# The last attention of an eight-stage block: both batch elements' head quartets in one branch, and the second element's projections, values and routing spread over it

## The chip, the cores and the metric

The kernel runs on one core of one Trainium2 chip. A core has five engines, each with an instruction stream of its own: TensorE (PE; its weight loads are shown as PEld), VectorE (DVE), ScalarE (ACT), GpSimd (POOL) and SyncE (SP), which here only issues DMAs. The metric is the device time of one execution in microseconds (us); lower is better. The time before is the median of three runs.

## The reference, cut to what matters

x has two elements of 512 tokens by 512 channels (float32). Eight stages follow one another, each as x = x + stage(layernorm(x)). Only the last two are touched: a causal attention of 32 heads of 16 channels with rotary positions, and a feed-forward stage in which a router picks two of eight low-rank experts for each token (this stage is also run ahead of the attention, with the same weights).

```python
def _L1_attn_b_ref(hidden_states, qkv_w, qkv_b, out_w, out_b):
    qkv = hidden_states @ qkv_w + qkv_b
    q, k, v = jnp.split(qkv, 3, axis=-1)          # 32 heads of 16
    q = _rope(q, cos, sin)
    k = _rope(k, cos, sin)
    scores = jnp.einsum('bqhd,bkhd->bhqk', q, k) * scale
    scores = scores + (1.0 - causal) * MASK_VAL   # -66504
    probs = jax.nn.softmax(scores, axis=-1)
    ctx = jnp.einsum('bhqk,bkhd->bqhd', probs, v).reshape(b, s, e)
    return ctx @ out_w + out_b

def _L1_ffn_ref(x, W_base, b_base, W_router, A, B):
    logits = x_flat @ W_router.T
    probs = jax.nn.softmax(logits, axis=-1)
    topk_probs, topk_idx = jax.lax.top_k(probs, 2)
    topk_probs = topk_probs / jnp.sum(topk_probs, axis=-1, keepdims=True)
    combine = jnp.einsum('nk,nke->ne', topk_probs, onehot)
    hw = jnp.einsum('nd,erd->ner', x_flat, A) * combine[:, :, None]
    return x_flat @ W_base.T + b_base + jnp.einsum('ner,eor->no', hw, B) * 2
```

## The kernel before, in words

Tokens lie in tiles of 128 (four to an element, t = 0..3 for element 0 and 4..7 for element 1), x stays in SBUF, and `xT[b]` holds the layernormed element b transposed, channels in partitions. A line number is that of the kernel before.

**Projections** (`prepare`, L1770). For element b, `rotated` (L1747) makes q and then k in four tiles of 128 channels (eight heads) by 512 tokens: a chain of four products on TensorE (L176), on ACT the bias (L1755), on DVE a shuffle of the halves of each head (L1757) and the product with the sine table into `t2` (L1758), on POOL the product with the cosine table (L1759) and the sum (L1760). `t2` is a tile of the pool's tag "qm". Then DMAs (L1764) store the tile's heads into `rooms.q` and `rooms.kk`, where a *quartet* u (four heads) has a plane of its own, each head in the first 16 of 32 partitions. A spare partition of every head carries the row maximum into the second score product. `values(b)` (L1781) makes v token tile by token tile; DVE adds the bias (L1785). Between q and k of element 0 come the layernorms of element 1's tiles; between q and k of element 1 comes `experts.begin()` (L1611): for the four tiles of element 0, whose attention is then complete, a layernorm, the added bias, and `front` (L1544), the router: one chain, and some fifteen small DVE instructions that end with the weighted rows `hw` (L1568).

**Quartets** (`core`, L1792). Each of the eight quartets of an element takes 16 scores (S; `score` L1813: TensorE, four widths of 128 to 512 keys; DVE adds the mask and reduces the row maximum, L1823), a transposition of these maxima (M; `maxima` L1837, and their sum with q on DVE, L1839), 16 transposed scores (T; `transposed` L1849, exponential on ACT L1859, the diagonal cut on POOL L1863), the product with v (`values` L1874, copied by ACT L1882), and a division (L1888 to L1892). After the eight quartets the context is transposed (L1906) and copied (L1910, DVE and ACT in turn) and multiplied by the output weights; `add_to_x` (L237) adds the result to x on DVE.

**What sets the order.** TensorE's order within `core` is written out by hand (`run_ordered`, L361): eight scores ahead, then for each quartet the string below, in which `|` is the division of the quartet before; scores run ahead of the quartet whose transposed scores are due, so 24 scores stand before the first T (the *fill*), and the last quartets of an element have no scores left to issue. The other engines' order, and that outside `core`, is set by a planner from the program's order and its costs. Scores, products and transpositions take the eight PSUM banks in turn (`turn`, BANKS).

```python
order = "STTSTSSTSTTSTSTSTTTTS|TTSTMTSSSSSS"
...
for b in range(B):
    prepare(b)
    with tc.If(exact != 0) as branch:
        core(b, True)
    with branch.Else():
        core(b, False)
```

`exact` tells at run time whether the masked scores can be left out; if not, the Else branch works on all of them. There is one such branch per element. After the second, `Experts.end` (L1618) runs `back` (L1577) for each tile of element 0, layernorms and routers of element 1, their `back`, and the stores of the result. `HeadRooms` (L1690) owns the planes of q, k and v, and fills their spare parts on POOL during the experts' first run.

Of the kernel before, what the change touches and what calls it, by code (L numbers as in the profile page):

```python
# [39 lines left out]
P = 128  # L40
NT = S // P
# [5 lines left out]
class Block:  # L47


    def __init__(self, ctx, tc, x, out):  # L50
# [10 lines left out]
        self.held = None  # L61
# [66 lines left out]
    def proj(self):  # L128
        return self.bank("pj", 2)

    def tr(self):
        return self.bank("tp", 2)

    def sc(self):
        return self.bank("sc", 3)

    def av(self):
        return self.bank("av", 1)
# [14 lines left out]
    def hold(self):  # L153


        self.holding = ExitStack()
# [6 lines left out]
    def release(self, ctx):  # L163
        self.holding.close()
        self.held = None
        self.psum = ctx.enter_context(
            self.tc.tile_pool(name="psum", bufs=2, space=bass.MemoryType.PSUM)
        )
# [1519 lines left out]
class HeadRooms:  # L1688
# [5 lines left out]
    def __init__(self, k, a, pool):  # L1694
# [9 lines left out]
        self.nm = [one([P, NT, P], f"nm{i}") for i in range(2)]  # L1704

    def fill(self, i):
        pool = self.k.nc.gpsimd
        pool.memset(self.q[:, i], 0.0)
# [6 lines left out]
def attn_mha(k, a, exact, rooms, experts):  # L1715
# [9 lines left out]
    with ExitStack() as ctx:  # L1725
# [8 lines left out]
        bv = k.load_row(a["h_bv"], D, "h_bv", pool=lp)  # L1734
# [3 lines left out]
        v_of = lambda kc, head: v[:, (kc * H + head) * 17 : (kc * H + head) * 17 + 32]  # L1738
# [7 lines left out]

        def rotated(b, w, bias, out, queues):  # L1747
# [3 lines left out]
            for tt in range(T):  # L1751
                ps = k.proj()
                last = k.chain(ps, [(w[:, c, bass.ts(tt, P)], k.xT[b][:, c]) for c in range(KC)])
                y = full[:, tt]
                nc.scalar.activation(y, ps, AF.Identity, bias=bias[:, tt : tt + 1], scale=1.0)  # L1755
                t2 = lp.tile([P, S], F32, tag="qm", name="t2")
                nc.vector.stream_shuffle(t2, y, swap)  # L1757
                nc.vector.tensor_tensor(t2, t2, tables["sin"], ALU.mult)  # L1758
                nc.gpsimd.tensor_tensor(y, y, tables["cos"], ALU.mult)  # L1759
                nc.gpsimd.tensor_tensor(y, y, t2, ALU.add)  # L1760
# [20 lines left out]
        def values(b):  # L1781
            for t in range(NT):
                ps = k.sc()
                k.chain(ps, [(k.xT[b][:, c, bass.ts(t, P)], wv[:, c]) for c in range(KC)])
                nc.vector.tensor_tensor(  # L1785
                    v[:, t * H * 17 : (t + 1) * H * 17].rearrange("p (h d) -> p h d", d=17)[:, :, 0:16],
                    ps.rearrange("p (h d) -> p h d", d=16),
                    bv.rearrange("p (h d) -> p h d", d=16),
                    ALU.add,
                )  # L1790

        def core(b, causal):  # L1792
# [3 lines left out]
            if not causal:  # L1796


                wide = S + (NT - 1) * P
                add = lp.tile([P, wide], F32, tag="add", name="add", bufs=1)  # L1800
                addT = lp.tile([P, wide], F32, tag="addT", name="addT", bufs=1)
                for m, sign in ((add, 1), (addT, -1)):
                    nc.gpsimd.memset(m, 0.0)
                    nc.gpsimd.affine_select(
                        out=m, in_=m, compare_op=ALU.is_ge, fill=masked,
                        base=sign * (S - P), pattern=[[-sign, wide]],
                        channel_multiplier=sign,
                    )

            def score(u, qt, g):  # L1810
                kv = (qt + 1) * P if causal else S
                ps = k.turn()
                nc.tensor.matmul(  # L1813
                    ps[:, :kv],
                    q[rows[g], u, bass.ts(qt, P)],
                    kk[rows[g], u, :kv],
                    start=True,
                    stop=True,
                )
                at = 32 * g + spare  # L1820
                lo = S - (qt + 1) * P
                mask = k.mask if causal else add
                nc.vector.tensor_tensor_reduce(  # L1823
                    out=ps[:, :kv],
                    in0=ps[:, :kv],
                    in1=mask[:, lo : lo + kv],
                    op0=ALU.add,
# [88 lines left out]
        for b in range(B):  # L1916
            prepare(b)
            with tc.If(exact != 0) as branch:
                core(b, True)
# [190 lines left out]
```

## Time and profile before

| | us |
|---|---|
| median of three runs | 2051.23 (2049.56 to 2051.96) |
| the profiled execution | 2050.64 |
| its span in the profile | 2048.9 |
| mean granted TensorE clock in it | 0.987 |
| first score of element 0 / of element 1, start | 1729.9 / 1898.2 |
| values of the eight quartets, element 0, first start and last end | 1749.1 / 1819.45 |
| the same, element 1 | 1916.4 / 1986.97 |
| output products of element 1, end | 2003.0 |

How the profile is read: times count from the start of the span. PE, DVE, ACT and POOL are the engines; a name with q (SPq) is an engine's DMA and control queue, PEld the weight loads of TensorE. L176 is a line of the kernel. An instruction's line shows its start, its duration, the operation, "out<-in" by the program's names with partitions x elements, how many, and in brackets the idle time of its engine before it and who ended that. A windows line shows a stretch, its length, then each engine's busy time and instructions, the granted TensorE clock (1.00 is full), the DMAs' share and GB/s.

### The profile page before, as it was taken

Reading aid. Unit: us, or ns where it says so; the run is one execution under the profiler, and the core shown is the slowest. Engines: PE = TensorE matmul, PEld = TensorE weight load, DVE = VectorE, ACT = ScalarE, POOL = GpSimd, SP = SyncE. Lnnn points to the kernel's source line nnn. Section 1 sums busy time; section 2 is a strip of 40 time slices with the busy share of each in tenths; the row PEclk is TensorE's granted clock in tenths of the full one; section 3 lists DMA queues with packets and bytes.
Section 4 is the critical chain, followed back from the end, with each engine's and each line's share of the span. In section 5 each row is a group of like instructions: output and inputs, shape, how many; then the busy total and the mean of one; then the engine's idle time right before and its main releaser. Section 6 shows DMA issues by size and latency. Waiting matters only on the chain. (4 is left out here: it accounts for less than half of the span.)

```text
span 2048.9 us, 39076 instructions
## 1 busy us (share of the span) xinstructions
PE 1974.3 (96%) x15064; PEld 1107.5 (54%) x15064; DVE 1333.1 (65%) x3510; ACT 759.0 (37%) x2094; POOL 1003.5 (49%) x1288
## 2 busy tenths in 40 slices
PE   9899989999999999999999999999999989997999
PEld 5333346666666666666665545454544544654654
DVE  8779657656665566566664586666666675845854
ACT  3776622222232223222222264454445211641451
POOL 4411046675645567666653266646555544225121
PEclk9999999999999999999999999999999999999999
DMA  3010222122221222222221321020101003002001
GB/s 136 11 42 1 73 74 85 56 78 90 95 74 51 80 76 82 77 92 79 73 86 40 115 66 47 2 76 2 62 12 43 6 6 47 2 2 36 7 2 42
DMA packets 69784, 108.85 MB, mean 53 GB/s; under 512 B 13522, under 2 KB 50386, under 8 KB 62548
## 3 DMA queue, kind: packets, MB, share of 16 engines
q1 hardware_dynamic: 68660, 103.10, 16.1%
q8 instruction: 122, 2.00, 0.4%
q10 hardware_dynamic: 640, 1.05, 0.3%
q0 software_dynamic: 288, 2.10, 0.3%
q14 instruction: 74, 0.61, 0.1%
HBM read 80.00 MB, written 4.19 MB: 41 GB/s over the span
## 5 line engine op out<-in xcount | busy, mean ns | idle before, releaser
L282 ACT ACTIVATE room<-room,nmax 128x128 f32<-128x128 f32 (+3 forms) x384 | 212.1, 554 | 481.7 <-DVE nmax L272 480.7
L261 PE MATMUL held<-kT,q 128*32 128x64 f32 (+15 forms) x4096 | 264.7, 397 | 15.2 <-DVE invs L290 12.4
L293 POOL TENSOR_SCALAR room<-room,invs 128x128 f32<-128x128 f32 (+3 forms) x384 | 198.3, 536 | 153.3 <-DVE invs L290 153.3
L176 PE MATMUL held<-w,ctxT 128*128 128x512 f32 x512 | 228.8, 595 | 0.1
L272 DVE CUSTOM_DVE_ANT_0 room<-held,mask 128x128 f32<-128x128 f32 (+3 forms) x384 | 176.0, 487 | 65.6 <-PE held L261 62.0
L261 PEld LDWEIGHTS held<-kT,q 128*32 128x32 f32 x4096 | 142.5, 110 | 106.5 <-issue 28.8
L333 PE MATMUL held<-turned,vals 32*128 32x384 f32 (+7 forms) x2784 | 192.8, 421 | 2.1 <-DMA vals<-v 2.1
L570 DVE TENSOR_REDUCE nm<-held 128x1 f32<-128x512 f32 x256 | 161.7, 683 | 32.2 <-PE held L600 26.6
L333 PEld LDWEIGHTS held<-turned,vals 32*128 32x128 f32 (+1 forms) x2784 | 153.2, 169 | 39.9 <-issue 18.9
L176 PEld LDWEIGHTS held<-w,ctxT 128*128 128x128 f32 x512 | 94.7, 190 | 115.8 <-issue 108.4
L237 DVE TENSOR_TENSOR x<-held,x 128x512 f32<-128x512 f32 x120 | 81.5, 684 | 114.9 <-PE held L176 95.0
L306 DVE STREAM_TRANSPOSE turned<-room 128x1152 f32<-128x1152 f32 x80 | 109.2, 1366 | 43.5 <-POOL room L293 40.0
L1067 POOL TENSOR_TENSOR q<-q,cosq 128x512 f32<-128x512 f32 x60 | 89.4, 1491 | 59.7 <-DVE t L1064 59.7
L176 PE MATMUL held<-fold,ctxT 128*128 128x512 f32 x256 | 117.8, 604 | 0.5 <-ACT ctxT L347 0.5
L229 POOL TENSOR_TENSOR rstd<-ve,mhalf 128x1 f32<-128x1 f32 x64 | 36.8, 579 | 160.6 <-DVE ve L227 160.6
L282 ACT ACTIVATE probs<-probs,nmax 128x128 f32<-128x128 f32 (+3 forms) x128 | 71.1, 556 | 67.3 <-DVE nmax L272 66.1
L1023 PE MATMUL held<-room,w 128*128 128x256 f32 x384 | 95.1, 384 | 0.0
L293 POOL TENSOR_SCALAR probs<-probs,invs 128x128 f32<-128x128 f32 (+3 forms) x128 | 66.0, 535 | 58.9 <-DVE invs L290 56.9
L176 PE MATMUL sc<-w,room 128*128 128x512 f32 x208 | 92.7, 592 | 0.0
L1068 POOL TENSOR_TENSOR q<-q,t 128x512 f32<-128x512 f32 x64 | 88.0, 1374 | 6.5 <-DVE q L1067 2.5
L305 DVE STREAM_TRANSPOSE turned<-room 128x128 f32<-128x128 f32 x80 | 24.3, 304 | 101.3 <-POOL room L293 101.1
L1023 PEld LDWEIGHTS held<-room,w 128*128 128x128 f32 x384 | 71.4, 190 | 32.3 <-issue 21.6
(333 smaller groups left out, 4425.0 us busy)
## 6 DMA issues: line engine op xcount, KB each, us to landing
w<-in_b_wq SPq DMA_DIRECT2D x16, 1024.0 KB, 4.8
w<-in_b_wo SPq DMA_DIRECT2D x16, 1024.0 KB, 5.0
vals<-v SPq DMA_DIRECT2D x256, 64.0 KB, 2.0
w<-in_m_wo SPq DMA_DIRECT2D x8, 1024.0 KB, 4.8
w<-in_b_wk SPq DMA_DIRECT2D x16, 256.0 KB, 2.6
w<-in_b_wupv SPq DMA_DIRECT2D x16, 256.0 KB, 2.6
w<-in_m_wqn SPq DMA_DIRECT2D x8, 384.0 KB, 3.0
x<-in_x SPq DMA_DIRECT2D x8, 256.0 KB, 4.1
```

The source lines that it names most:

```text
L176: last = self.nc.tensor.matmul(out, lhsT, rhs, start=(i == 0), stop=(i == len(pairs) - 1))
L237: self.latest = self.nc.vector.tensor_tensor(self.x[t], ps, self.x[t], ALU.add).ins
L261: nc.tensor.matmul(ps[32 * i : 32 * i + 32, a - lo : b - lo], q[:, at : at + 32], keys[:, a:b], start=True, stop=True,)
L272: nc.vector.tensor_tensor_reduce(out=row, in0=ps[:, :kv], in1=self.mask_back[:, :kv] if qt % 2 else self.mask[:, S - kv :], op0=ALU.add, o ...
L282: nc.scalar.activation(row, row, AF.Exp, bias=nmax, scale=-1.0, accum_out=total[:, qt : qt + 1])
L293: self.nc.gpsimd.tensor_scalar(row, row, inv[:, qt : qt + 1], 1.0, ALU.mult, ALU.mult)
L306: self.nc.vector.transpose(out[:, :last], probs[:, :last])
L333: self.nc.tensor.matmul(out[:, :, :n], values(i, j), rhs, start=(j == blocks[0]), stop=(j == stop[i]),)
L570: k.latest = nc.vector.tensor_reduce(nm[u % 2][:, qt, at : at + 1], ps, AX.X, ALU.max, negate=True).ins
L1023: nc.tensor.matmul(out, lhsT[:, c], rhs[:, c], start=c == 0, stop=c == 1)
L1067: mul.tensor_tensor(q, q, tables["cosq"], ALU.mult)
L1068: nc.gpsimd.tensor_tensor(q, q, t2, ALU.add)
```

## The change

In the causal branch both elements' quartets run as one list of sixteen, n = 0..15, in one branch, which also holds `Experts.end`; the second `If` and all that stood between the two is gone from between them. The Else branch holds both elements one after the other, as before.

- `k.hold()` after `prepare(0)`: from there all eight banks are one held tile, and `proj`, `tr` and `sc` take the next bank in turn. `t2` takes the two buffers of the layernorm's "xn" instead of those of "qm".
- `HeadRooms` has four more planes (`more`), for q and k of the second element's first two quartets; the others reuse planes whose quartet of element 0 is done (`place`). POOL fills them in the experts' first run, with two memsets and two copies.
- The fill: two scores, then a projection tile of element 1, four times (q and k for heads 0 to 15), sixteen stores to `more` after the first two, ten scores, the maxima, six scores. The other sixteen stores of these tiles are issued after quartet 1.
- After quartet 7, `between`: the four remaining projection tiles with three scores after each and 32 stores, maxima of quartet 9, POOL's memsets of the places of element 1's v (in the space of wq and wk), the division, the first v tile, three scores, the context's transposition of element 0, its four output products with two scores after each, then three v tiles, the four layernorms and three of the four routers. The fourth router comes after quartet 8.
- The rotated tiles of element 1 lie in `xT[0]`, and so does the turned context of element 0: the four copies of the context follow the stores of the four tiles of `between`.
- Quartets 0 to 7 carry 16 scores each, and the maxima one quartet ahead; quartets 8 to 15 carry what is left, with the maxima two ahead.

The diff, cut to its core:

```diff
     def proj(self):
-        return self.bank("pj", 2)
+        return self.bank("pj", 2) if self.held is None else self.turn()
...
+        self.more = one([P, 4, S], "more")
...
+        def turn_pairs(y, ps, bias):
+            nc.scalar.activation(y, ps, AF.Identity, bias=bias, scale=1.0)
+            t2 = k.work.tile([P, S], F32, tag="xn", name="t2")
+            nc.vector.stream_shuffle(t2, y, swap)
+            nc.vector.tensor_tensor(t2, t2, tables["sin"], ALU.mult)
+            nc.gpsimd.tensor_tensor(y, y, tables["cos"], ALU.mult)
+            nc.gpsimd.tensor_tensor(y, y, t2, ALU.add)
...
+            flat = lambda w: w.rearrange("p c d -> p (c d)")
+            late, last = flat(wq)[:, : 3 * H * 17 + 32], flat(wk)[:, : H * 17 + 32]
+            ctxT = k.xT[0], wv
+            place = lambda b, u: u if b == 0 else u - 2 if u > 1 else 8 + u
+            q_of = lambda n: q[:, n] if n < 8 else rooms.more[:, n - 8]
+            k_of = lambda n: kk[:, n] if n < 8 else rooms.more[:, n - 6]
...
+            ys = [k.xT[0][:, i] for i in range(4)]
+            stored = {}
+
+            def rotated_tile(kind, tt):
+                w, bias = (wq, bq) if kind == "q" else (wk, bk)
+                ps = k.turn()
+                k.chain(ps, [(w[:, c, bass.ts(tt, P)], k.xT[1][:, c]) for c in range(KC)])
+                y = ys[(2 * tt + (kind == "k")) % 4]
+                turn_pairs(y, ps, bias[:, tt : tt + 1])
+                stored[kind, tt] = y
+
+            def store(tt):
+                for kind, of in (("q", q_of), ("k", k_of)):
+                    y = stored.pop((kind, tt))
+                    for n in range(8):
+                        at = 32 * (n % 4)
+                        nc.sync.dma_start(
+                            out=held(1, 2 * tt + n // 4, of)[at : at + 16],
+                            in_=y[16 * n : 16 * n + 16],
+                        )
...
+            def between():
...
+                for tt in (2, 3):
+                    for kind in "qk":
+                        rotated_tile(kind, tt)
+                        next_scores(3)
+                    store(tt)
+                maxima(9)
+                nc.gpsimd.memset(late, 1.0)
+                nc.gpsimd.memset(last, 1.0)
+                divided(7)
+                value_tile(0)
+                next_scores(3)
+                for c in range(T):
+                    turn_context(ctxts[0], ctxT[0], c)
+                for t in range(NT):
+                    output(0, t)
+                    next_scores(2)
+                experts.added = experts.bias()
+                for t in range(NT):
+                    if t:
+                        value_tile(t)
+                        next_scores(1)
+                    k.layernorm(t, bias=experts.added)
+                    if t:
+                        experts.front(t - 1)
+
+            ORDER = "STTSTSSTSTTSTSTSTTTTS|TTSTMTSSSSSS", "STTSTSSTSTTSTSTSTTTTS|TTSTTMSSSSSS"
             with tc.manual_schedule(engines={mybir.EngineType.PE}):
...
+                for tt in range(2):
+                    for kind in "qk":
+                        next_scores(2)
+                        rotated_tile(kind, tt)
+                    if tt == 0:
+                        store(0)
+                next_scores(10)
+                maxima(0)
+                next_scores(6)
+                for n in range(16):
...
+                    values_of(n)
+                    if n == 1:
+                        store(1)
+                    if n == 7:
+                        between()
+                    if n == 8:
+                        experts.front(NT - 1)
+                divided(15)
...
+            experts.end()
+
+        prepare(0)
+        k.hold()
+        with tc.If(exact != 0) as branch:
+            causal()
+        with branch.Else():
+            core(0)
+            prepare(1)
+            core(1)
+            experts.end()
```

## The prediction

> **What bounds the kernel now.** I read the page's busy shares first: TensorE is busy 96% of the span, so only two things can shorten it, less work on TensorE (the change removes none) or less of the 4% in which it stands.
>
> ```profile
> PE 1974.3 (96%) x15064; PEld 1107.5 (54%) x15064; DVE 1333.1 (65%) x3510; ACT 759.0 (37%) x2094; POOL 1003.5 (49%) x1288
> ```
>
> Then the windows view, cut at the stages of the last attention. Columns: stretch, length, busy time and instructions of each engine, granted TensorE clock, DMA share, GB/s.
>
> ```profile
> 1686.90:1729.90 43.00, 42.92 (x111) 19.32 (x111) 16.61 (x33) 7.52 (x12) 28.77 (x20) 1.00 0.36 55
> 1729.90:1740.10 10.20, 7.68 (x54) 5.51 (x56) 9.76 (x43) 0.00 (x0) 0.00 (x0) 0.81 0.02 4
> 1740.10:1821.40 81.30, 80.92 (x795) 49.71 (x791) 60.45 (x240) 49.76 (x137) 20.40 (x32) 0.98 0.01 2
> ...
> 1835.50:1849.30 13.80, 13.80 (x34) 6.07 (x33) 8.62 (x21) 2.06 (x3) 7.81 (x8) 1.00 0.01 2
> 1849.30:1868.90 19.60, 8.15 (x50) 7.17 (x48) 17.11 (x67) 3.69 (x9) 11.13 (x9) 0.83 0.37 52
> 1868.90:1884.30 15.40, 15.40 (x32) 6.69 (x33) 5.45 (x16) 2.06 (x3) 7.65 (x5) 0.89 0.03 3
> 1884.30:1898.20 13.90, 13.90 (x37) 5.91 (x35) 3.51 (x6) 0.69 (x1) 4.54 (x4) 1.00 0.51 77
> 1898.20:1908.60 10.40, 8.00 (x60) 6.00 (x62) 10.31 (x47) 0.00 (x0) 0.00 (x0) 0.92 0.00 0
> ```
>
> They are: projections of element 0; its fill (24 scores before the first transposed score); its eight quartets; then, for element 1, q projection, layernorms with routers, k projection, v, fill. Both fills run at DVE's pace (9.76 of 10.20), and in the routers' stretch TensorE stands 19.60 - 8.15 = 11.45 us while DVE works 17.11. The waits view says the same of the routers:
>
> ```profile
> PE pj L176 <- DVE cand L1537: 10.2, 2, 7.7
> ```
>
> What can be won is thus 11.45 (routers) + 2.4 (second fill) + 15.4 - 13.8 = 1.6 (the k projection at a clock of 0.89), some 15 us. The first fill stays.
>
> **The change part by part.** Unit prices: a projection tile is one chain of 13.8/4 = 3.45 us on TensorE; values start every 10.12 us in the quartets that issue 16 scores, 9.58 with half, 7.85 without; DVE takes 0.25, 0.385, 0.515, 0.65 us for a score of width 128 to 512 (7.2 per quartet), 0.69 for qm, 0.75 for a division: 8.65 of 10.12. All in us, against the profiled execution.
>
> 1. *Projections of element 0.* The rotation's second tile (t2) now shares its two buffers with layernorm's xn. The xn of the sixth token tile waits for q3's add on POOL, queued behind a bias add (1.27); TensorE, in order, waits for that xn's transposes inside the k chains. I take **+3.0**; 0 if the planner's cover holds, +4 if it waits for the whole POOL queue.
>
> 2. *Hold.* All banks become one held tile behind their old readers; the first score waits for the last v add (0.69 us) and its handover: **+0.9** (0 to 1.5).
>
> 3. *Fill.* Four chains of element 1 come in, 13.8 on TensorE. DVE could have hidden them, had the 24 scores come with them; but only 8 narrow scores (2.5 us of DVE) stand among the chains. Each tile costs DVE a shuffle and a product:
>
> ```profile
> 1694.10 0.69 ACT L1755 ACTIVATE room<-pj,h_bq 128x512 f32<-128x512 f32 x1 [2.69 <-PE pj L176]
> 1694.83 0.73 DVE L1757 STREAM_SHUFFLE t<-room 128x512 f32<-128x512 f32 x1
> 1695.59 0.69 DVE L1758 TENSOR_TENSOR t<-t,w 128x512 f32<-128x512 f32 x1
> ```
>
> (start, duration, idle time before). The last chain ends 13.8 + about 1.6 = 15.4 after the core's start. k1's activation (0.7), its shuffle and product (1.4) and the last eight scores of quartet 0 (4 x 0.515 + 4 x 0.65 = 4.7) are still ahead of the first maxima: 22.2; its transposes 0.6, qm 0.7 and the handovers 0.7 bring the first transposed score to 24.2 instead of 10.2: **+14.0**. So these chains are only moved. Bounds: +10 if DVE catches up in the first quartets, +16 with the products slowed. For that slowing the row is 1.75 us for the same product beside a POOL product, against 0.69 alone:
>
> ```profile
> 1854.06 1.75 DVE L1758 TENSOR_TENSOR t<-t,w 128x512 f32<-128x512 f32 x1
> ```
>
> The Trainium skill, page "SBUF — State Buffer", section "Who interferes with whom", says that a DVE instruction with two SBUF inputs contends with a GpSimd instruction that reads SBUF. The two rows agree; the rule speaks against this change, which sets more rotations (POOL) beside DVE's work. If it struck all eight moved products, the sum would be 8 x 1.06 = 8.5 us of DVE worse, by estimate; scores read PSUM and one SBUF mask, so I take none of it.
>
> 4. *Quartets 0 to 7.* All issue 16 scores, where the seventh issued half and the eighth none: (10.12 - 9.58) + (10.12 - 7.85) = **+2.8** (0 to 4). These scores are gone later.
>
> 5. *Between the halves.* Before: from the last values of element 0 (end 1819.45) to the first transposed score of element 1 (1907.55), 88.1. After: TensorE has 12 chains (q2, k2, q3, k3, four v, four output), 41.3; 26 scores, 7.9; maxima 0.6, division 0.6, context transposes 1.8, four layernorms' transposes 1.8, three routers 2.8: 56.8. Layernorms and routers hide beside the v chains (DVE: about 2.9 per router, 1.4 per layernorm, against 3.45 plus a score). What is late next are the stores. q2 to k3 lie where the turned context goes, so its copies wait until each has been stored, by eight DMAs each on SP, 32 in all. The nearest rows for the issue are SBUF to SBUF DMAs of the same engine:
>
> ```profile
> 1171.86 10.37 SPq L356 DMA_DIRECT2D vals<-turned  x16
> ...
> 1199.04 10.68 SPq L356 DMA_DIRECT2D vals<-room  x16
> ```
>
> That is 0.65 us per issue (0.60 to 0.79 in other groups: 8 in 6.35 for q's stores); landing 2.0 (the same vals stores on the page). q2's add ends 3.45 + 4.9 = 8.4 after the start (ACT, DVE, POOL as in the rows of point 3, POOL 1.77 + 1.27); 32 issues bring the last landing to 8.4 + 20.8 + 1.3 = 30.5, the fourth copy to 31.2. TensorE needs that copy for output(0,0)'s fourth product, at 27.1 by the same list of work. **Stall 4.2**, and 1.5 for the lower clock after it (the fill's window shows 0.81 after a stop). Sum 56.8 + 5.7 = 62.5: **-25.6**. Bounds of the stall: 0 (issues hidden) and 14 (see the slow rival).
>
> The Trainium skill, page "DMA: Bandwidth & Descriptors", section "Issuing engines are not separate DMA queues", says that issuing on several engines only saves the sequencer's issue time, "which is usually small relative to the DMA itself". Here the row differs: sixteen issues took 10.37 us, the landing of one 2.0. By the rule the stall and its clock would be gone, and the sum 5.7 lower.
>
> 6. *Second half.* 178 of 256 scores were issued earlier (24 + 8 x 16 + 26); the 78 left fill 4.9 quartets, where 104 filled 6.5: 1.6 x 2.27 = 3.7 less. But routers 2 and 3 fall here: 2.9 us of DVE each, of which 1.5 is slack in a quartet, and 0.93 on TensorE: 2 x 2.3 = 4.6 more, **+0.9** (-4 if they hide, +6 if the bank that each holds meanwhile stops TensorE too).
>
> 7. *End.* No branch edge ahead of the experts' second run; TensorE's wait there goes (DVE's first instruction after the edge comes 2.12 late, TensorE loses 0.82):
>
> ```profile
> 2006.06 0.69 DVE L191 BATCH_NORM_STATS2 ln_stats<-x 128x6 f32<-128x512 f32 x1 [2.12 <-issue]
> ...
> 2008.42 0.66 PE L214 MATMUL tp<-ident,xn 128*128 128x128 f32 x4 [0.82 <-DVE xn L201]
> ```
>
> **-0.8**; the jump over the other branch at the very end costs 0 to 0.5. The two memsets and two copies on POOL in the experts' first run (under 0.65 each) lie beside a TensorE that is busy there: nothing; without that cover 2.3.
>
> Sum: 3.0 + 0.9 + 14.0 + 2.8 - 25.6 + 0.9 - 0.8 = **-4.8**: 2050.64 - 4.8 = 2045.8 for the profiled execution, 2046.4 against the median of the runs shown, 2051.23, which lies 0.6 above it.
>
> **The rivals.**
> *A, clearly faster.* DVE catches up in the first quartets (fill +10.5 instead of 14) and the stores stay hidden (no stall, 5.7 less): -4.8 - 3.5 - 5.7 = -14.0: 2037; with the one alone 2041 to 2043. For it: DVE is idle 1.5 us per quartet, and the quartets' window shows TensorE at 80.92 of 81.30. Against it: the maxima must wait for all 16 of a quartet's scores, in the fill as before.
>
> *B, slower: the stores.* Place: the context copies before output(0,0). If the 32 issues go at the 0.79 of q's stores (6.35/8) and land like the slowest of these, 7.2 us after issue, the fourth copy comes at 8.4 + 25.3 + 7.2 - 0.8 + 0.6 = 40.7, a stall of 13.6 instead of 4.2, and the clock after a stop so long (0.73 to 0.89 in the windows after the routers) costs another 2 to 4: -4.8 + 9.4 + 3 = +7.6: 2059. It decides from a stall of about 11 us, where the sum passes +4.1. For it: this row of stores from the same tile shape in before.
>
> ```profile
> 1706.96 6.35 SPq L1764 DMA_DIRECT2D qs<-room  x8
> ```
>
> Against it: those stores carried 128 KB each, the new ones 32 KB.
>
> *C, nothing:* what the fill gives the branch takes, -4 to +4: 2047 to 2055. Of this kind too would be that the change does not do what it says, the planner setting the moved work elsewhere; TensorE's order is written out by hand in the branch, so only prepare(0) is open to that. The other branch is not run: the trace of before has scores of widths 128 to 512, which only the first has.
>
> **How the numbers follow.** Forecast 2046.4, own range 2041 to 2051, chance 0.50, of which 0.28 lies below 2047.1 (faster by over 0.2%, 4.1 us, about what a measurement of this kernel can tell from no change). A: 0.22, all faster. C beyond the forecast's own range: 0.10, same. B: 0.18, slower. Faster 0.50, same 0.32, slower 0.18. The range, 2036 to 2057, takes in most of A and, with the upper bounds of points 3 and 6, nearly half of B's spread (2055 to 2060); some 0.16 is left out.
>
> **What would show it.** First transposed score 24 us after the first score (20 or less speaks for A); a TensorE wait of 3 in the k chains of element 0; SP issuing 32 stores without a gap between the halves, and TensorE at its output chain waiting for a copy that waits for SP: 4 us (B: over 11; A: none); 62 us from the last values of quartet 7 to the first transposed score of quartet 8, counted from 0; routers' bank waits in the two quartets after. Wrong I would be if DVE, not TensorE, set the pace of the quartets with the second element's scores in them, or if the stores landed out of step with their issue.

## The result, and the profile after

The kernel after took 2071.75 us (median; the six runs on record lie between 2066.46 and 2082.94), the kernel before 2050.39 in the same session: a ratio of 1.0118, 95% interval 1.0078 to 1.0158. It is about 21 us slower, where 5 us faster was forecast, and outside the range. The profiled execution of the kernel after is the second longest of the six: 2081.45 us, span 2079.7, at a mean granted clock of 0.976; the two runs at the median ran at 0.981. So the stages below add up to 30.8 us, and some 10 of them are clock that the median does not pay (an estimate, span times one minus clock: 49.9 us at 0.976, 39.3 at 0.981).

The windows view of the kernel after, cut at the first score, the first transposed score, the last values of quartet 7, the first transposed score of quartet 8, and the last values (columns as before: length, busy time of each engine, granted clock, DMA share, GB/s):

```profile
1692.40:1742.73 50.33, 46.36 (x112) 21.47 (x113) 18.99 (x35) 7.85 (x12) 30.27 (x21) 0.93 0.31 47
1742.73:1769.15 26.42, 22.20 (x86) 10.54 (x89) 17.16 (x54) 2.75 (x4) 10.64 (x8) 0.89 0.09 21
1769.15:1852.33 83.18, 82.38 (x831) 51.11 (x826) 69.67 (x286) 49.13 (x135) 20.40 (x32) 0.97 0.04 8
1852.33:1921.84 69.51, 65.16 (x214) 28.95 (x214) 39.37 (x125) 7.39 (x13) 19.80 (x18) 0.93 0.07 16
1921.84:2018.02 96.18, 91.36 (x729) 52.06 (x728) 52.50 (x208) 49.56 (x137) 20.40 (x32) 0.86 0.01 1
2018.02:2079.70 61.68, 56.84 (x188) 29.32 (x188) 26.38 (x96) 7.01 (x19) 7.28 (x8) 1.00 0.10 36
```

The second half of the kernel before, in the same view:

```profile
1907.55:1986.97 79.42, 79.05 (x779) 48.33 (x775) 59.52 (x240) 48.90 (x135) 20.40 (x32) 0.98 0.01 2
```

The same stages of both kernels, and what was forecast for each:

| stage | before | after | difference | forecast |
|---|---|---|---|---|
| up to the experts' first router (untouched code) | 1633.3 | 1637.0 | +3.8 | 0 |
| experts' first run | 53.7 | 55.4 | +1.7 | 0 |
| projections of element 0, with the hold | 43.0 | 50.3 | +7.4 | +3.9 |
| fill | 10.2 | 26.4 | +16.2 | +14.0 |
| quartets 0 to 7 | 79.4 | 83.2 | +3.8 | +2.8 |
| between the halves | 88.1 | 69.5 | -18.6 | -25.6 |
| second half | 79.5 | 96.2 | **+16.7** | **+0.9** |
| end | 61.9 | 61.7 | -0.2 | -0.8 |

The first row is no part of the change: over all kernels of this study, whose code is the same there, it took 1633.3 to 1638.8. The row that failed is the second half. In the window line it has TensorE busy 91.36 us at a clock of 0.86, while the kernel before needed 79.5 for the same quartets at 0.98.

The page of the kernel after says the same of the whole:

```profile
PE 2002.0 (96%) x15064; PEld 1111.2 (53%) x15064; DVE 1337.3 (64%) x3510; ACT 760.1 (37%) x2094; POOL 1005.2 (48%) x1294
```

TensorE's busy time rose by 27.7 us, from 1974.3 to 2002.0, with the same 15064 instructions, and its share is 96% as before. So most of the 30.8 us is not standing: the same products took longer.

The waits view of the kernel after, TensorE only, from 1690 us on (engine, tile and line; what it waited for; us in total, times, the longest):

```profile
PE held L1968 <- DVE hw L1568: 4.5, 2, 2.3
PE held L176 <- ACT room L1907: 4.3, 1, 4.3
PE held L1956 <- DVE nm L1877: 3.6, 2, 2.1
PE tp L214 <- DVE xn L201: 2.9, 1, 2.9
PE held L1934 <- DMA bias<-in_f_bias: 1.1, 1, 1.1
```

From the top: a transposed score (L1968) needs the bank that a late router still holds, twice; the output product of element 0 waits for ACT's copy of the context, which follows the stores; the fill's maxima, for DVE's reduced scores; the layernorm tile in the projections; the hold. Together 16.4 us, of which the forecast had the stops of 4.2, 3.0 and 0.9, and had priced the routers' 4.5 as 4.6 of work.

What the forecast did not have is behind the stops. The windows view again, around the two late routers:

```profile
1921.00:1926.00 5.00, 2.73 (x27) 1.97 (x29) 3.57 (x23) 2.43 (x5) 0.00 (x0) 1.00 0.01 2
1926.00:1930.00 4.00, 3.96 (x33) 3.27 (x28) 2.31 (x10) 2.96 (x9) 1.28 (x2) 0.67 0.02 4
1930.00:1934.80 4.80, 4.80 (x25) 2.28 (x23) 2.21 (x6) 1.27 (x6) 1.27 (x2) 0.50 0.00 0
1934.80:1940.00 5.20, 5.20 (x49) 2.53 (x50) 3.10 (x13) 0.60 (x2) 0.00 (x0) 0.73 0.00 0
1940.00:1945.00 5.00, 2.75 (x29) 1.76 (x22) 4.07 (x25) 2.25 (x5) 0.00 (x0) 0.94 0.02 3
1945.00:1954.50 9.50, 9.50 (x47) 5.54 (x42) 4.68 (x16) 3.86 (x13) 2.55 (x4) 0.50 0.00 0
1954.50:1965.90 11.40, 11.40 (x106) 6.78 (x104) 8.91 (x36) 6.29 (x17) 2.55 (x4) 0.99 0.01 1
```

In the first and fifth lines TensorE is busy 2.7 of 5 us: the stops. After each, the clock stands at one half for about ten microseconds although TensorE is busy throughout. The last line is quartet 10 at full clock, without a stop, and it takes 11.4 us where its like took 10.12 before: a third effect, neither stop nor clock.

The Trainium skill, page "TensorE: Matmul & The Clock Gate", part 1, gives the gate two states, full and half, judged over free-running windows of about 3.4 us, with one idle window to fall. This case shows the two states, and its stretches at half clock last 3.4, 6.8, 10.2 or 13.7 us, which fits windows of that length; but here the clock fell after stops of 2.25 us, shorter than one window.

A smaller effect stands in the fill. These are two of its four products with the sine table on DVE (L1757) and POOL's products with the cosine table beside them (L1758):

```profile
1748.67 0.69 DVE L1757 TENSOR_TENSOR t<-t,w 128x512 f32<-128x512 f32 x1
1748.71 1.77 POOL L1758 TENSOR_TENSOR room<-room,w 128x512 f32<-128x512 f32 x1 [16.01 <-DVE t L1756]
...
1752.86 1.27 POOL L1758 TENSOR_TENSOR room<-room,w 128x512 f32<-128x512 f32 x1 [1.03 <-DVE t L1756]
1753.03 1.65 DVE L1757 TENSOR_TENSOR t<-t,w 128x512 f32<-128x512 f32 x1
```

In these rows the one that starts second is the long one. Three of the fill's four DVE products took 1.65, 1.65 and 1.51 us in place of 0.69, and three of the four between the halves took 1.38 to 1.78.

### The profile page after: what moved, and what is told of

Same layout as the page of the kernel before. It is cut to its first block, busy times and chain, and to the rows that moved or that the text cites. A ratio compares the mean times of both kernels' runs of the same rounds, so it can differ in the third digit from the quotient of the medians.

```text
span 2079.7 us, 39188 instructions
## 1 busy us (share of the span) xinstructions
PE 2002.0 (96%) x15064; PEld 1111.2 (53%) x15064; DVE 1337.3 (64%) x3510; ACT 760.1 (37%) x2094; POOL 1005.2 (48%) x1294
## 4 chain that ended last, share of the span: by engine, by line
PE 87%; DVE 6%; POOL 3%; issue 1%; ACT 1%; DMA 1%; SPq 1%; POOLq 0%; DVEq 0%; ACTq 0%
PE held L176 28%; PE held L261 11%; PE held L333 9%; PE held L1023 9%; PE held L1934 3%; PE held L1968 3%; PE held L610 3%; PE held L964 3%; PE held L562 2%; PE held L1991 2%; PE held L447 2%; PE held L1345 2%; DVE nm L570 2%; PE pj L176 1%; PE held L1342 1%
## 5 line engine op out<-in xcount | busy, mean ns | idle before, releaser
L272 DVE CUSTOM_DVE_ANT_0 room<-held,mask 128x128 f32<-128x128 f32 (+3 forms) x384 | 175.9, 487 | 65.2 <-PE held L261 61.7
L237 DVE TENSOR_TENSOR x<-held,x 128x512 f32<-128x512 f32 x136 | 92.6, 685 | 153.7 <-PE held L176 130.1
L1877 DVE CUSTOM_DVE_ANT_0 held<-held,mask 128x128 f32<-128x128 f32 (+3 forms) x256 | 119.2, 519 | 44.0 <-PE held L1934 40.7
L1934 PE MATMUL held<-ks,qs 32*128 32x128 f32 (+3 forms) x448 | 95.0, 513 | 1.9 <-DMA bias<-in_f_bias 1.1
L176 PE MATMUL held<-w,room 128*128 128x512 f32 (+2 forms) x256 | 89.0, 494 | 5.0 <-ACT room L1907 4.3
```

The lines of the kernel that those rows point to most:

```text
L176: last = self.nc.tensor.matmul(out, lhsT, rhs, start=(i == 0), stop=(i == len(pairs) - 1))
L237: self.latest = self.nc.vector.tensor_tensor(self.x[t], ps, self.x[t], ALU.add).ins
L272: nc.vector.tensor_tensor_reduce(out=row, in0=ps[:, :kv], in1=self.mask_back[:, :kv] if qt % 2 else self.mask[:, S - kv :], op0=ALU.add, o ...
L1877: nc.vector.tensor_tensor_reduce(out=ps, in0=ps, in1=mask, op0=ALU.add, op1=ALU.max, scale=1.0, scalar=-3e38, accum_out=nm[u % 2][:, qt, a ...
L1934: nc.tensor.matmul(ps, held(b, u, q_of)[rows[g], bass.ts(qt, P)], held(b, u, k_of)[rows[g], :kv], start=True, stop=True,)
```

## The experiments

There were twelve more kernels, and none leaves out any of the work; each is compared with the kernel before on its own chip. Stage times are those of each kernel's one profile.

**The kernel after, again.** No edit.

> The changed kernel once more, unchanged, to see which of its stretches at half clock are its own. Theory: they follow TensorE's stops, so half clock shows again after the same five stops (2.9 us in the projections of element 0, 2.2 before the first maxima, 4.3 at the output product of element 0, 2.3 and 2.2 behind the two late routers), 3 to 10 us long each, and the kernel is 0.5 to 1.5% slower than before. Rival (the clock falls on its own, by chance): the stops are there again, but half clock shows in other places, and full clock after at least three of the five.

Ratio 1.0104 (1.0076 to 1.0133). The stops came at the same places and lengths (2.89, 2.29, 4.18, 2.25, 2.25). The clock fell again behind the context's copies (4.8 us lost, as length times one minus clock) and in the second half (15.6 lost), but not behind the 2.89 in the projections: 47.5 us at a clock of 1.00, against 50.3 at 0.93. The five later profiles with that stop lost 1.5 to 1.9 there. So part of the rival holds: in the projections the size of the loss differs from run to run. In the quartets the clock fell after both late routers in both profiles; an exception follows below.

**168 scores ahead of quartet 8.**

```diff
                 value_tile(0)
-                next_scores(3)
...
                     output(0, t)
-                    next_scores(2)
+                    next_scores(1)
...
                         value_tile(t)
-                        next_scores(1)
```

> Ten scores fewer between the halves, so that quartet 8 begins with 168 scores issued (8 past a multiple of 16, as in the first half) in place of 178 (2 past it). Theory: the 11.4 us of quartets 9 to 11 come from the wide scores falling into the run of six at the end of the order; with the offset of the first half these quartets take 10.0 to 10.3 at full clock. Rival (the quartets of the second half are dearer in themselves, by the v in the weights' place or the maxima two ahead): they stay at 11.2 to 11.5. In the whole: minus 3 to minus 4 us by the first, and between plus 1 and minus 1 by the second.

Ratio 1.0055 (1.0035 to 1.0075). Quartets 10 and 11 start 10.21 us before the next, in place of 11.36 and 11.15 (quartet 9 begins at the lower clock behind a router, 11.23). So the offset is the cause, and the rival falls. The reason given for it covers only a part. With 178 scores issued, each quartet of the second half begins with the third score of a group of sixteen: the narrow ones fall beside the wide transposed scores, and the four widest, 0.65 us each on DVE, into the run of six at the end. But from the start of the maxima to the start of the values, where that run stands, a quartet takes 1.87 us with 178 and 1.44 with 168: 0.43 of the 1.15. The other 0.72 lie ahead of the maxima, and what makes them stays open. In the whole the gain, 11.3 us between the medians of one session, is larger than the 3 to 4 forecast: the ten scores also left the stretch between (65.0 after 69.3), and this profile lost 10.0 us to the clock in the second half, where the others lost 13.5 and 15.6.

**The last two routers at the output products of element 1.**

```diff
                     k.layernorm(t, bias=experts.added)
-                    if t:
+                    if t in (1, 2):
                         experts.front(t - 1)
...
-                    if n == 8:
-                        experts.front(NT - 1)
...
                     output(1, t)
+                    if t < 2:
+                        experts.front(t + 2)
```

> The third and fourth router go from the start of the second half to the output products of element 1, where a chain of 3.4 us follows each. Theory: TensorE's two stops of 2.3 and 2.2 us go, and with them the half clock after each (some 5 us each in the changed kernel's profile): minus 8 to minus 14 us. Rival (a stop costs its own length only): minus 4 to minus 5, with half clock in the second half as before.

Ratio 1.0065 (1.0043 to 1.0086), 10.8 us under the kernel after in the same session (2064.95 and 2075.74, medians). Both stops are gone, and the second half takes 84.9 us with 5.1 lost to the clock, where the kernel after took 96.2 and 97.7 with 13.5 and 15.6 lost. The theory holds; the stops of 4.5 us and the routers' chains, priced at 0.93 each, make 6.4 of the 11.3 to 12.8 us by which the stage shortened, so the rival falls. The quartets without stops still take 11.36.

**The rotation's buffers in the projections.**

```diff
-        def turn_pairs(y, ps, bias):
+        def turn_pairs(y, ps, bias, place=(k.work, "xn")):
...
-            t2 = k.work.tile([P, S], F32, tag="xn", name="t2")
+            t2 = place[0].tile([P, S], F32, tag=place[1], name="t2")
...
-                turn_pairs(full[:, tt], ps, bias[:, tt : tt + 1])
+                turn_pairs(full[:, tt], ps, bias[:, tt : tt + 1], (lp, "qm"))
```

> The rotation's second tile has its old buffers again in the projections of element 0 (in the branch it shares with the layernorm as in the changed kernel). Theory: the stop of 2.9 us at the transposes there goes, and the half clock after it: the projections take 43 to 44 us in place of 50.3, minus 6 to minus 7 in the whole. Rival (stop only): 47 us, minus 3. Second rival (the added copies and the hold make the stage longer, not the shared buffers): no change.

Ratio 1.011 (1.0087 to 1.0134): in the whole nothing that can be told from the kernel after. In its profile the stage is as the theory has it:

```profile
1688.60:1732.70 44.10, 42.97 (x108) 19.32 (x109) 17.25 (x34) 7.47 (x12) 28.74 (x20) 1.00 0.35 53
```

44.1 us, the 43.0 of before and the hold's 1.1. The shared buffers cost 2.9 us, and 0 to 3.5 of clock by the run; the 6 to 7 us that the theory gave the whole were not seen.

**The context in free planes.** Planes 6 and 7 of q and k are read last by quartet 7.

```diff
-            ctxT = k.xT[0], wv
+            ctxT = [q[:, 6], q[:, 7], kk[:, 6], kk[:, 7]], [wv[:, i] for i in range(T)]
```

> The turned context of element 0 goes to planes 6 and 7 of q and k, which are free after quartet 7, so that its copies no longer follow the 32 stores. Theory: the stop of 4.2 to 4.3 us at the first output product goes, and with it the half clock behind it (4.8 us lost in the stretch between the halves): that stretch takes 60 to 61 us in place of 69.3, minus 9 in the whole. Rival (the clock falls in this stretch anyway): minus 4. Second rival (the copies waited for something else than the stores): no change.

Ratio 1.0073 (1.005 to 1.0097). The stretch between the halves, in its profile:

```profile
1847.10:1907.70 60.60, 60.59 (x216) 27.78 (x213) 39.17 (x125) 7.39 (x13) 19.77 (x18) 1.00 0.08 18
```

TensorE does not stop, the clock is full, and 69.3 to 69.5 us have become 60.6: the stop and the clock loss, 9 us, were both the stores'. The stores themselves are as forecast; the last of SyncE's queue in the kernel after (start, duration, number), and the copy behind them:

```profile
1871.53 5.01 SPq L2023 DMA_DIRECT2D qs<-room  x8
1876.64 5.55 SPq L2023 DMA_DIRECT2D ks<-room  x8
...
1883.91 0.59 ACT L1907 COPY room<-held 128x512 f32<-128x512 f32 x1 [6.87 <-DMA ks<-room]
```

0.63 and 0.69 us each, the last issue over at 1882.2; the copy follows its landing, and TensorE went on at 1884.55. The forecast set the Trainium skill's page "DMA: Bandwidth & Descriptors", section "Issuing engines are not separate DMA queues", which calls issue time usually small relative to the DMA, against this price. The measurement sides with the price taken from the row: an issue is here a third of the 1.9 us to a store's landing, and 32 of them stood in a row.

This kernel also has the exception. Its late-router stops are still there, but after the first of them, of 2.25 us, the clock stayed at full:

```profile
1909.00:1911.50 2.50, 0.27 (x4) 0.00 (x1) 2.32 (x16) 1.57 (x3) 0.00 (x0) 1.00 0.01 3
1911.50:1917.00 5.50, 5.43 (x46) 3.91 (x50) 4.26 (x17) 3.92 (x13) 2.27 (x4) 1.00 0.01 3
```

Six profiles have both stops, of 2.25 to 2.81 us. Half clock came after eleven of the twelve, for 10.2 us in eight cases, 13.7 in two and 3.4 in one. So such a stop mostly lowers the clock here, but not always.

**The fill without tiles.**

```diff
-                for tt in range(2):
-                    for kind in "qk":
-                        next_scores(2)
-                        rotated_tile(kind, tt)
-                    if tt == 0:
-                        store(0)
-                next_scores(10)
+                next_scores(18)
                 maxima(0)
...
                     values_of(n)
-                    if n == 1:
-                        store(1)
+                    if n < 4:
+                        rotated_tile("qk"[n % 2], n // 2)
+                    if n in (1, 3):
+                        store(n // 2)
```

> The four projection tiles of the fill go to the ends of quartets 0 to 3, one each; the fill is that of the kernel before. Theory: the fill takes 10.2 us again in place of 26.4, and DVE's slack hides the rotations in the quartets, whose four pitches grow by 3.4 each from 10.2: minus 16.2 plus 13.8, minus 2 to minus 3 in the whole. Rival (DVE sets the pace of the quartets, so that a tile costs its rotation too): pitches of 14.5 to 15, plus 2 to 4 in the whole.

Ratio 1.0139 (1.0118 to 1.016). The fill is back at 9.85 us, but the quartets with a tile take 15.1:

```profile
1741.60:1751.45 9.85, 8.01 (x53) 6.60 (x56) 9.08 (x42) 0.00 (x0) 0.00 (x0) 0.61 0.01 4
1760.21:1775.31 15.10, 14.77 (x113) 7.86 (x114) 9.89 (x41) 7.19 (x18) 5.55 (x7) 1.00 0.05 10
1775.31:1790.75 15.44, 14.76 (x112) 7.84 (x113) 9.88 (x41) 7.19 (x18) 5.88 (x7) 1.00 0.09 20
```

A tile of 3.4 us costs 4.9 there: fill and quartets 0 to 7 together take 112.5 in place of 109.4 to 109.6. The rival holds in its pitches, though DVE is busy only 9.9 of 15.1; the next kernel shows why.

**All cures, one tile after each quartet.**

```diff
-        if i < 2:
-            pool.memset(self.more[:, i], 0.0)
+        if 4 <= i < 6:
+            pool.memset(self.more[:, i - 4], 0.0)
...
+                next_scores(18)
+                turned = rotated_tile("q", 0)
                 maxima(0)
+                turned()
...
                     values_of(n)
+                    if n < 7:
+                        rotated_tile("kq"[n % 2], (n + 1) // 2)()
+                        if n % 2 == 0:
+                            store(n // 2)
```

The four cures above are in it, and 16 scores between the halves, where no tiles are left; `rotated_tile` now gives back its rotation, to be run where it is called.

> All cures at once: old buffers in the projections, context in planes 6 and 7, the spare planes filled beside the later tiles of the experts' first run, one tile of element 1 in the fill ahead of the maxima and one after each of quartets 0 to 6, 16 scores between the halves, the last two routers at the output products of element 1. Theory: projections 44, fill 12, quartets 0 to 7 107, between 39 to 42, second half 78 to 80, end 64: 345 us against 362 in the kernel before, minus 14 to minus 18, about 2036 where the kernel before takes 2052. Rival (the branch in itself or the tiles among the quartets cost what the stops did): within 5 us of the kernel before.

Ratio 0.9991 (0.9977 to 1.0006): no change against the kernel before, and 12 us above the theory: the rival's number. Projections 44.1, between 40.8, second half 75.8 and end 64.0 came as expected or better; the miss is quartets 0 to 7, 120.6 in place of 107. DVE behind quartet 2 (with the bracket: idle time before it, and who ended it):

```profile
1791.82 0.57 DVE L1877 CUSTOM_DVE_ANT_0 held<-held,mask 128x384 f32<-128x384 f32 x1 [4.97 <-PE held L1934]
...
1792.31 0.01 DVE L1756 LOAD_MASK_SELECT t<-room  x1
1792.31 0.76 DVE L1756 STREAM_SHUFFLE t<-room 128x512 f32<-128x512 f32 x1
1793.11 0.69 DVE L1757 TENSOR_TENSOR t<-t,w 128x512 f32<-128x512 f32 x1
1793.72 0.56 DVE L1877 CUSTOM_DVE_ANT_0 held<-held,mask 128x384 f32<-128x384 f32 x1
```

DVE stands 4.97 us while TensorE does the values and the tile, and then runs the rotation among the scores, whose pace it sets.

**A stop alone.** In the kernel before, behind the maxima of quartets 2 and 4:

```diff
                 nc.vector.tensor_tensor(t, tp, q[:, u], ALU.add)
+                if causal and u in (2, 4):
+                    for _ in range(9):
+                        nc.vector.tensor_tensor(t, t, t, ALU.max)
```

> The kernel before, with nine needless DVE instructions of 0.69 us (a maximum of the shifted q with itself) behind the maxima of quartets 2 and 4 of each element, so that TensorE stops there for 2 to 3 us in full work and nothing else is changed. Theory: the clock is halved for 3 to 10 us after such a stop, so each costs 3 to 5 us beyond its length (four stops: 24 us in all with their own 10). Rival: the clock stays at 1.00 after most of them, and the whole costs the stops' own length.

One run, 2086.02 us, where the kernel before took 2050.11: 36 us more, and 24 was the theory. The stops came out longer than meant, 4.87 us each, and the four quartets took 17.81, 17.55, 17.28 and 17.07 us in place of 10.12: 2.1 to 2.8 us beyond the stop, 29 us in all; the other 7 lie outside these quartets and are one run's. Around the first (windows view):

```profile
1766.00:1770.00 4.00, 1.29 (x17) 0.45 (x6) 4.00 (x15) 0.58 (x1) 0.00 (x0) 1.00 0.00 0
1770.00:1772.00 2.00, 0.00 (x0) 0.00 (x0) 1.93 (x5) 0.00 (x0) 0.00 (x0) 0.86 0.00 0
1772.00:1778.00 6.00, 5.83 (x31) 4.54 (x34) 2.94 (x10) 3.17 (x7) 0.64 (x1) 0.50 0.00 1
1778.00:1780.00 2.00, 1.79 (x22) 1.28 (x18) 1.86 (x7) 1.50 (x6) 0.63 (x1) 0.93 0.00 0
1780.00:1784.00 4.00, 3.99 (x58) 2.33 (x58) 3.67 (x19) 1.14 (x5) 1.27 (x2) 1.00 0.00 0
```

The clock falls during the stop, stays at one half for 6 us of full work, and comes back. All four stops show it, with half clock for 3.4 to 6.8 us. So a stop of this length lowers the clock by itself, in the kernel before too; its price beyond its length was 2.1 to 2.8 us where I expected 3 to 5. Stops of 2.25 us were not tried alone.

**The tile ahead of the values.**

```diff
+                    if n < 7:
+                        rotated_tile("kq"[n % 2], (n + 1) // 2)()
+                        if n % 2 == 0:
+                            store(n // 2)
                     values_of(n)
-                    if n < 7:
-                        rotated_tile("kq"[n % 2], (n + 1) // 2)()
-                        if n % 2 == 0:
-                            store(n // 2)
```

> The version with all cures, and each of its seven tiles ahead of its quartet's values product in place of behind it. Theory: behind it, DVE stood 4.97 us through the product and the tile and then ran the rotation (1.45 us) among the scores whose pace it sets; ahead of it, the rotation falls beside the product, so the pitches of quartets 0 to 6 go from 15.1 to 13.6 to 13.8 us: minus 9 to minus 11 in the whole, 2037 to 2039 where the kernel before takes 2050. Rival (a tile of 3.4 us takes 5 wherever it stands, by the banks it blocks): pitches of 15 and no change.

Ratio 0.9942 (0.9925 to 0.9959). The pitches are 13.62 to 13.97. The same place on DVE:

```profile
1790.25 0.74 DVE L1756 STREAM_SHUFFLE t<-room 128x512 f32<-128x512 f32 x1
1791.03 0.69 DVE L1757 TENSOR_TENSOR t<-t,w 128x512 f32<-128x512 f32 x1
1792.56 0.57 DVE L1877 CUSTOM_DVE_ANT_0 held<-held,mask 128x384 f32<-128x384 f32 x1 [0.84 <-PE held L1934]
```

The rotation is done before the first wide score. Nothing but the place of seven chains changed, and a tile costs 3.4 to 3.8 us again.

**Covers for the divisions.** The first v tile goes ahead of division 7, a second one behind it, the third router ahead of division 15.

```diff
-                divided(7)
                 value_tile(0)
+                divided(7)
                 next_scores(4)
+                value_tile(1)
...
+                experts.front(2)
                 divided(15)
```

> The same, with TensorE work between the last values of each element and its division (the first v tile, the third router), and a second v tile ahead of the output products. Theory: TensorE's waits of 0.7 (twice) and 0.9 us go: minus 2 us against the version with the tiles ahead. Rival (the layernorms, which lose the second v tile as their cover, stop TensorE by as much): no change.

2030.85 us, ratio 0.9915 (0.9895 to 0.9936): the fastest kernel here, 0.85% under the kernel before. The waits of 0.7, 0.9 and 0.7 us are gone; the stretch between went from 40.8 to 39.5, and the end from 63.8 to 63.0. Against that, the second half took 77.8 in place of 75.9: the clock stood at one half for 3.4 us in its last quartet. The intervals of this kernel and the last overlap, so only those two stage times speak for the 2 us. The profile is of a run of 2038.49 us at a clock of 0.987; four of the six took 2029.93 to 2031.08 at 0.992 to 0.994, so part of the median's gain may be clock.

**The two cures of the second half alone.** The edits of the second and third experiment together.

> The changed kernel with the two cures of its second half alone: 168 scores ahead of quartet 8, and the last two routers at the output products of element 1. Theory (their effects add): the second half, 96.2 to 97.7 us in the changed kernel, takes 77 to 80 at full clock, as was forecast for it, and the whole stands 3 to 8 us above the kernel before, by the stops that are left. Rival (one hides the other, or the clock falls in quartets 12 to 14 also without a stop before): 84 us or more.

Ratio 1.002 (1.0001 to 1.0038). The second half takes 75.8 us at a clock of 1.00. Three of its quartets:

```profile
1931.50:1941.70 10.20, 10.20 (x106) 6.61 (x104) 8.53 (x37) 6.07 (x17) 2.54 (x4) 1.00 0.00 0
1941.70:1951.90 10.20, 10.20 (x106) 6.60 (x104) 8.54 (x37) 6.08 (x17) 2.54 (x4) 1.00 0.01 2
1951.90:1962.10 10.20, 10.20 (x106) 6.60 (x104) 8.53 (x37) 6.08 (x17) 2.54 (x4) 1.00 0.01 2
```

The two edits take the kernel after to within 0.4% of the kernel before. In the profiles the second half gave 20.4 to 21.9 us of it; the stretch between, which the ten scores left, gave 5, and the end, which now has the routers, took 2 back.

**Four cures, the fill as the change has it.** The same with the old buffers and the context in free planes.

> The same, and the old buffers in the projections of element 0 and the context in planes 6 and 7: all stops gone but the one of the hold and those of the fill, whose tiles stay where the change has them. Theory: projections 44.1, fill 26.4, quartets 0 to 7 83, between 54 to 57, second half 77 to 80, end 64: 350 to 353 against 362 in the kernel before, but 1.6 more in the experts' first run: minus 7 to minus 10, about 2042. Rival (without the fill's tiles moved there is no gain): 2048 to 2053.

2041.6 us, ratio 0.9955 (0.9935 to 0.9974). Projections 44.1, fill 26.4, quartets 0 to 7 83.2, between 54.9, second half 75.8, end 63.6: 348 against 362. The rival falls: the tiles in the fill cost the same 16.2 us as in the kernel after, and with the four cures the change gains 9 us without moving them.

## Why the prediction was wrong, step by step

- *What bounds the kernel.* "Only two things can shorten it", less work or less standing, left out the third: how fast the work runs. TensorE stayed busy 96% of the span and took 27.7 us longer for the same instructions.
- *Projections (1) and hold (2).* Right: stops of 2.89 and 1.09 us, forecast 3.0 and 0.9. The lower clock behind the first was left out (0 to 3.5 us).
- *Fill (3).* Right in kind, 16.2 for 14.0. The chains are moved, not hidden. Two sizes make up the 2.2: the last chain ended 16.8 us after the first score, not 15.4, and k1's product with the sine took 1.51 us, not 0.69. That slowing had a row and an upper bound of +16 in the forecast, which then took none of it; and its row of "0.69 alone" was not alone, for a POOL product started 0.05 us after it and took 1.77. Between the halves the slow products, with the stores' stop gone, stopped TensorE nowhere.
- *Quartets 0 to 7 (4).* Right: 3.6 to 3.8 for 2.8; the pitch with hold is 10.19 for 10.12.
- *Between (5).* The stop was 4.2 to 4.3 us as forecast, and it goes with its cause. The stop's size came from the stores as worked out; two other terms were mis-sized. "1.5 for the lower clock after it" was 4.9 in this profile. And "26 scores, 7.9" is 12: the stretch without stops takes 60.6 us with 26 scores and three routers, and 54.9 with 16 and two, so a score that stands alone between chains costs (5.7 - 0.93)/10 = 0.47 us, not 0.30.
- *Second half (6).* **The step that failed**: "+0.9 (-4 if they hide, +6 if the bank that each holds meanwhile stops TensorE too)". The bank did stop TensorE, twice, 2.25 us: the upper bound's mechanism. What it lacked was the half clock after the stops and the offset of the scores. The first, as measured: moving the routers took 11.3 to 12.8 us off the second half, where their work and stops had been priced at 4.6, and put some 2 onto the end. The second: 1.15 us per quartet, three to four quartets. With both gone the stage takes 75.8, which is the 3.7 us of saving that the step began with.
- *End (7).* No gain, -0.2 for -0.8: the wait of 0.82 at the edge went, and one of 0.71 for ACT's copy of the last values came ahead of division 15.
- *POOL's copies.* "Nothing" was wrong by 1.7 us: the experts' first run took 55.3 to 55.8 in every kernel with the spare planes' filling beside its first tiles, 55.0, 55.0 and 54.3 with it beside the later ones, 53.6 and 53.7 without it. Why the later place cures only some of it is open.
- *Rivals.* B, the slow one, was wrong: the stores stopped TensorE by 4.3, not by over 11. A was wrong as well, and so was C, which ended at 2055. The side was B's, the mechanism a fourth one.

The clock also fell in quartets 13 and 14, where no stop over 0.5 us shows ahead of it: pitches of 10.1 and 7.85 in place of 7.85 twice, in the kernel after and in every experiment that kept 178 scores (8.8 and 9.5 in the one with the context in free planes), and in none with 168. (With 168 it also fell for 3.4 us in quartet 15 of two kernels, the one with that edit alone and the one with covers for the divisions.) Its cause stays open, and it is a part of the clock that stops do not explain.

## What to carry to other kernels

On an engine that is 96% busy, ask whether its busy time itself will grow, and price a stop at its length and the half clock behind it: in the quartets mostly 2 to 5 us more. A small reduction that holds a PSUM bank, such as a router, stopped nothing here ahead of chains of 3.4 us, and stopped TensorE by 2.25 ahead of short products that go round all banks. When work is set among a hand-written order, ask where the neighbouring engine is idle in that order: the same tile cost 4.9 us behind the values and 3.4 to 3.8 ahead of them, and the same scores 11.4 or 10.2 us by the offset at which they entered.

## What the runs showed that I had not expected

- Stops of 2.25 us were enough, eleven times of twelve, to halve the clock in quartets, where products use 32 rows, mostly for about ten microseconds; the stops of 4.87 us in the kernel before were followed by 3.4 to 6.8 us. After the 2.89 us stop among full chains 0 to 3.5 us were lost, by the run.
- The whole kernel's time goes with the clock: the six runs of the kernel after lie between 2066.46 us at 0.985 and 2082.94 at 0.975, 16 us apart with nothing in the code changed.
- The same DVE product with the sine table took 0.69 us or 1.38 to 1.79 in the kernel after, beside POOL's rotations; in the rows shown it was long where POOL's product had started first.
